# Five layers in one kernel: cross attention and layer 2 under one written TensorE order over five items, with shared PSUM pairs

## The chip, the cores and the metric

The kernel runs on one core of one Trainium2 chip. The time is the device time of one execution in microseconds (us); the kernel's time is the median over its runs. The inputs lie in device memory at the start, and the program is one launch.

In this text PE is TensorE, DVE is VectorE, ACT is ScalarE, POOL is GpSimd and SP is the engine that issues most DMAs.

## The reference, cut to what matters

The input `x` has 8 batches of 256 tokens by 320 channels; `ctx_768` holds 120 context tokens of 192 channels for each batch. Five blocks follow each other on the same `x`: a block with quantised attention and a feed-forward layer (L0), a plain transformer block (L1: self attention, cross attention, feed-forward), an attention on text and image tokens (L2), and a last attention (L3). All is float32 with softmax over scores.

The change touches the cross attention of L1 and all of L2:

```python
# L1, cross attention (20 heads of 16)
h2 = _ln(x, n2_g, n2_b)
x = _attn(h2, context, q2, k2, v2, o2_w, o2_b, heads) + x
# L2: 104 text tokens and 16 image tokens, softmax for each set
q = (hidden_states @ Wq).reshape(B, S, H, D)
out = _attend(q, k, v, scale)
out_ip = _attend(q, k_ip, v_ip, scale)
out = (out + IP_SCALE * out_ip).reshape(B, S, C)
out = out @ Wo + bo
return out + residual
```

## The kernel before, in words

`x` stays in SBUF as 16 tiles of 128 tokens; a batch is two of them (`TPB`). L0's attention runs first, in stages of its own. From there on the kernel is one flow of 40 items, which `run_flow` interleaves: 4 feed-forward items of L0 (512 tokens each), then for each of the 8 batches one item of self attention, then 8 of cross attention, 4 of L1's feed-forward, 8 of L2, and 8 of the last attention.

An attention item has four generators: `project`, `tops`, `out` and a fourth that ends the output projection. At each step of `run_flow`, item `step + 1` does its `tops`, item `step + 2` its `project`, item `step - 1` its last part and item `step` its `out`; the generators are advanced in turn, one piece each. So four batches are in flight, and the engines' order comes from this interleaving and from the framework, which places the instructions on each engine's queue and adds the semaphores. PE's order is not fixed by hand except inside a feed-forward item (`behind`).

For cross attention (`kind == "cross"`) and L2 (`kind == "both"`), keys and values of the context were computed earlier and lie in DRAM (`kd`, `vd`). One item does this:

- `project`: normalises the batch (cross only; DVE L314 to L322), turns it by six PE transposes (`turned`, L339) into `xT` with ACT evacuation (L341, L343 or L347), loads keys and values by DMA (L523, L524), and computes the queries in one PSUM pair (`duo`, L132 for 128 rows, L139 for 64 rows), which ACT puts into `qT` (`put_q`, L360, L362). The 20 heads are padded to 32 rows and stand as five groups (`G`) of four, so a matmul with 32 rows runs for four heads side by side.
- `tops` (`max_scores`, L394, then DVE's maxima, L401): scores with tokens on the partitions, only for the negated maximum of each row. Two groups share two PSUM pairs (`per = 512 // (2 * 120) = 2`). Then PE turns the maxima (L418), ACT copies them into `nT` (L419), and SP writes them by DMA into spare rows of `qT` (L422), five DMAs for cross, ten for L2, so that the next scores come out with the maximum taken off.
- `out` (`weighted`): scores with keys on the partitions (L439), two groups in two pairs, ACT's exponential into `e` (L445), the product with the values and the sums with a matrix of ones (L456) in a single PSUM bank, DVE's reciprocal and product (L464, L465) into `oT`. Cross adds two groups in one bank; L2 has one group in a bank, with text and image in the two halves of a head's 32 rows.
- the output projection (`project_out_steps`): POOL adds the bias to `x` (L487), PE multiplies by the weights for each half of the tokens (L120; three chunks for cross, five for L2), DVE adds the result to `x` (L493).

PSUM has two pools: `pair()` gives one of 3 tiles of two banks (`pf` in the profile) and `bank()` one of 2 tiles of one bank (`pa`).

Of the kernel before, what the change touches and what calls it, by code (L numbers as in the profile page):

```python
# [2 lines left out]

# [8 lines left out]
F32 = mybir.dt.float32  # L12
BF16 = mybir.dt.bfloat16
AF = mybir.ActivationFunctionType
ALU = mybir.AluOpType
AX = mybir.AxisListType
PSUM = bass.MemoryType.PSUM

P = 128
B, N, C = 8, 256, 320  # L20
NT = B * N // P
TPB = N // P
M, CC = 120, 192
# [9 lines left out]
H, D, PAD = 20, 16, 32  # L33
G = H * PAD // P
NIP = 16
NTXT = M - NIP
# [18 lines left out]
class Kernel:  # L55
# [56 lines left out]
    def bias_row(self, pool, i):  # L112
        t = pool.tile([P, C], F32, tag="brow", name="brow", bufs=3)
        self.nc.scalar.dma_start(t, self.a["rows"][i : i + 1, :].to_broadcast([P, C]))
        return t

    def mm(self, out, pairs):

        for i, (l, r) in enumerate(pairs):
            self.nc.tensor.matmul(out, l, r, start=i == 0, stop=i == len(pairs) - 1)  # L120
# [39 lines left out]
    def open_flow(self, ctx):  # L160
        nc, tc = self.nc, self.tc
        self.ps_f = ctx.enter_context(tc.tile_pool(name="ps_f", bufs=3, space=PSUM))
        self.ps_a = ctx.enter_context(tc.tile_pool(name="ps_a", bufs=2, space=PSUM))
        self.fw = ctx.enter_context(tc.tile_pool(name="f_weights", bufs=1))
        self.fk = fk = ctx.enter_context(tc.tile_pool(name="f_keep", bufs=1))
        self.work = ctx.enter_context(tc.tile_pool(name="f_work", bufs=2))

        self.m32 = fk.tile([P, PAD], F32, name="m32")
        nc.vector.tensor_reduce(self.m32, self.ident.rearrange("p (j r) -> p r j", r=PAD), AX.X, ALU.add)
        self.half = fk.tile([P, 2], F32, name="half")  # L170
        nc.vector.tensor_reduce(self.half, self.m32.rearrange("p (s r) -> p s r", s=2), AX.X, ALU.add)

        self.magic = fk.tile([P, 4], F32, name="magic")
        nc.gpsimd.memset(self.magic[:, 0:1], MAGIC)
        nc.gpsimd.memset(self.magic[:, 1:2], -MAGIC)
        nc.vector.tensor_scalar(self.magic[:, 2:4], self.half, -MAGIC, None, ALU.mult)
        self.count = 0

    def open_quant(self, pool):

# [327 lines left out]
    def heads_item(self, b, ln, w, brow, kind):  # L508

        nc = self.nc  # L510
        it = {}

        def project():
            xT = self.work.tile([P, 3, N], F32, tag="xT", name="xT")
            self.normed_T(b, xT, 0, ln)
            it["q"] = qT = self.hp.tile([P, G, N], F32, tag="qT", name="qT", bufs=3)
            nk = N if kind == "self" else M
            kT = self.hp.tile([P, G * N], F32, tag="kT", name="kT", bufs=3)[:, : G * nk]
            it["k"] = kT = kT.rearrange("p (g k) -> p g k", k=nk)
            it["v"] = v = self.vs[self.count % 3]  # L520
            self.count += 1
            if kind != "self":
                nc.sync.dma_start(kT, self.kd[kind][:, b])  # L523
                nc.sync.dma_start(v[:M, 0], self.vd[kind][:M, b])  # L524
            yield
            two = lambda wt, m, n: [self.by_weight(wt[i], xT, m[i], i) for i in range(n)]
            yield
            if kind == "self":
                for n, put in (("q", lambda p: self.put_q(qT, p)), ("k", lambda p: self.put_k(kT, p))):
                    ps = self.pair()  # L530
                    self.duo([ps[:, m, :N] for m in range(2)], two((w[n], w[n]), (0, 1), 2))
                    put(ps[:, :, :N])
                    yield
                ps = self.pair()
                self.duo([ps[:, i, :N] for i in range(2)], two((w["q"], w["k"]), (2, 2), 2))
                self.put_q(qT, None, ps[:, 0, :N])
                self.put_k(kT, None, ps[:, 1, :N])
                yield
                ps = self.pair()
                self.duo([ps[:, t, :C] for t in range(TPB)], [self.by_token(w["v"], xT, t, t) for t in range(TPB)])  # L540
                self.put_v(v, ps[:, :, :C])
                return
            ps = self.pair()
            outs, terms = [ps[:, m, :N] for m in range(2)], two((w["q"], w["q"]), (0, 1), 2)
            last = [ps[:, 0, N:]], two((w["q"],), (2,), 1)
            self.duo(outs, terms)
            self.half_rows(*last, False, False)
            yield
            self.whole_rows(*last, False, True)
            self.put_q(qT, ps[:, :, :N], ps[:, 0, N:])  # L550

        def tops():
            segs = [(0, N)] if kind == "self" else [(0, M)] if kind == "cross" else [(0, NTXT), (NTXT, M)]
            yield from self.top_scores(it["q"], it["k"], segs[-1][1], segs)

        def out():
            both = kind == "both"

            def oT():
                if "oT" not in it and both:  # L560
                    t = self.hp.tile([P, 4, 512], F32, tag="big", name="oT2", bufs=4)
                    it["oT"] = t.rearrange("p a n -> p (a n)")[:, : G * N].rearrange("p (g n) -> p g n", n=N)
                elif "oT" not in it:
                    it["oT"] = self.work.tile([P, 3, N], F32, tag="oT", name="oT", bufs=1)
                return it["oT"]

            kc, ks = (TPB, P) if kind == "self" else (1, M)
            yield from self.weighted(it["q"], it["k"], it["v"], kc, ks, both, oT)
            it["out"] = self.project_out_steps(b, it["oT"], w["o"], brow, self.bank)
            next(it["out"])  # L570

        return project, tops, out, lambda: it["out"]

    def ff_item(self, blk, ln, which, func, w, brow):
        nc = self.nc
# [99 lines left out]
    def run_flow(self, items, before={}, after={}):  # L675


        n = len(items)
        made = {}
        for step in range(-2, n + 1):  # L680
            if step + 2 < n:
                if step + 2 in before:
                    before[step + 2]()
                made[step + 2] = items[step + 2]()
            order = ((step + 1, 1), (step + 2, 0), (step - 1, 3), (step, 2))
            gens = [made[i][k]() for i, k in order if 0 <= i < n]
            while gens:
                for g in list(gens):
                    try:
                        next(g)  # L690
                    except StopIteration:
                        gens.remove(g)
            if step in after:
                after[step]()

# [254 lines left out]
    def last_item(self, b, w, brow, to):  # L950
# [3 lines left out]
        nc = self.nc  # L954
        HT = H3 * T3
        scale = D3 ** -0.5
        it = {}

        def project():
            x = self.x[:, TPB * b : TPB * (b + 1), :]  # L960
            xT = self.work.tile([P, 3, N], F32, tag="xT", name="xT")
            self.turned(x, xT, 0)
            qT = it["q"] = self.hp.tile([P, G3, N], F32, tag="qT", name="qT3", bufs=3)
            kz = self.hp.tile([P, G * N], F32, tag="kT", name="kz", bufs=3)
            kT = it["k"] = kz[:, : G3 * K3].rearrange("p (g k) -> p g k", k=K3)
            z = it["z"] = kz[:, 512 : 512 + 2 * N].rearrange("p (g n) -> p g n", n=N)
            vu = self.vs[self.count % 3].rearrange("p t h d -> p (t h d)")
            self.count += 1
            v = it["v"] = vu[:, : H3 * PAD3].rearrange("p (h d) -> p h d", d=PAD3)
            u = it["u"] = vu[:, 512 : 512 + TPB * H3 * PAD].rearrange("p (t h r) -> p t h r", h=H3, r=PAD)  # L970
            cs = it["c"] = w["pool"].tile([P, 2, CC], F32, tag="cs", name="cs", bufs=3)
# [18 lines left out]
            ps = self.pair()  # L990
# [12 lines left out]
            ps = self.pair()  # L1003
            wz = w["z"].rearrange("p c h r -> p c (h r)")
            self.duo([ps[:, g, :N] for g in range(2)], [self.by_weight(wz, xT, g, g) for g in range(2)])
            for c, t in ((2, 0), (2, 1), (0, 0), (1, 0), (0, 1), (1, 1)):
                o, nh = N + 3 * c * HT, 4 if c < 2 else 2
                rows = slice(64 * t, 64 * (t + 1)) if c == 2 else slice(0, P)
# [3 lines left out]
                    skip_group_check=True,  # L1012
# [624 lines left out]
def kernel(ctx: ExitStack, tc: tile.TileContext, a, out):  # L1637
    k = Kernel(ctx, tc, a, out)
    with ExitStack() as es:
# [12 lines left out]
        w, brow, loaded, w3 = {}, {}, {}, {}  # L1652
        dram = es.enter_context(tc.tile_pool(name="ahead", bufs=1, space=bass.MemoryType.DRAM))
        ff = ExitStack()
        with tc.tile_pool(name="l0", bufs=1) as pool:
            k.open_quant(pool)
            with tc.tile_pool(name="l0_keys", bufs=1, side="right") as kpool:
                s = Quant(k, pool, kpool, 0, *load("L0", "Wq1", "Wk1", "Wv1", "Wo1", 0), False)
                k.load_ctx()
                s.project_all()  # L1660
                c = Quant(k, pool, pool, 1, *load("L0", "Wq2", "Wk2", "Wv2", "Wo2", 1), True)
# [6 lines left out]
                n = len(s.units)  # L1668
# [4 lines left out]
                v = c.values_all()  # L1673
# [60 lines left out]

        items = [lambda i=i: k.ff_item(i, 2, 0, AF.Gelu_apprx_tanh, loaded["w"], brow["ff0"]) for i in range(4)]
        items += [lambda b=b: k.heads_item(b, 3, w["self"], brow["self"], "self") for b in range(B)]
        items += [lambda b=b: k.heads_item(b, 4, w["cross"], brow["cross"], "cross") for b in range(B)]
        items += [lambda i=i: k.ff_item(i, 5, 1, AF.Gelu, loaded["w1"], brow["ff1"]) for i in range(4)]
        items += [lambda b=b: k.heads_item(b, None, w["both"], brow["both"], "both") for b in range(B)]
        items += [lambda b=b: k.last_item(b, w3, brow["last"], out) for b in range(B)]  # L1740
        before = {12: load_cross, 24: load_both}
        k.run_flow(items, before, {
# [80 lines left out]
```

## Time and profile before

| | us |
|---|---|
| median of 3 runs | 2204.13 |
| the runs | 2198.03, 2204.13, 2205.01 |
| span of the profiled execution | 2202.1 |

The page gives no other time for the profiled execution than its span; the span is 2.0 us under the median of the runs.

In the profile, an instruction's line is the line of the helper that records it; `out<-in` are the program's names. PEld is PE's weight load. One float32 matmul is shown as two records, so `x8` of a 32-row matmul is four heads once. A group's "idle before" is the time its engine stood idle just before it, with what ended that. PEclk is the granted TensorE clock as a share of full speed.

In the trace of before the feed-forward of L0 runs from about 650 us, self attention from about 960, cross attention from about 1230, the feed-forward of L1 from about 1425, L2 from about 1714 and the last attention from about 1925 to the end.

### The profile page before, as it was taken

To read this page: it belongs to the slowest core of one execution; us is meant where nothing else is said; L and a number is where in the kernel's file an instruction comes from. 1 tells how busy PE (TensorE), PEld (TensorE's weight loads), DVE (VectorE), ACT (ScalarE), POOL (GpSimd) and SP (SyncE) were. 2 spreads that over 40 slices of the span, in tenths; PEclk is the share of its full clock that TensorE was granted. 3 is DMA by queue.
4 is the path that set the end of the run, shared out by engine and by line. 5 is a ranking of instruction groups with operands and counts; after the bars stand their busy time and mean duration, and the time that the engine had idled before them with its cause. 6 is when DMAs were issued, how large, how long until landed. Compare 5 with 4: busy or idle time off the path is not lost.

```text
span 2202.1 us, 38254 instructions
## 1 busy us (share of the span) xinstructions
PE 2036.4 (92%) x16415; PEld 1194.6 (54%) x16415; DVE 1112.6 (51%) x1698; ACT 833.3 (38%) x1259; POOL 330.5 (15%) x358
## 2 busy tenths in 40 slices
PE   7888889898889999999999998899999999999997
PEld 5643345554444465465555555544555655666664
DVE  5388687445651222235555567621121666546565
ACT  3456888367542121124444444311201333222221
POOL 3194033723010000000000010100000100000100
PEclk9989889898899999999999999999999999999999
DMA  4000000642120000020000101100000120000000
GB/s 118 20 12 2 2 1 1 174 111 57 52 85 14 1 0 1 1 93 2 2 2 22 28 25 36 47 1 0 1 0 1 24 68 23 19 16 26 23 19 16
DMA packets 79303, 63.21 MB, mean 29 GB/s; under 512 B 48410, under 2 KB 68318, under 8 KB 78622
## 3 DMA queue, kind: packets, MB, share of 16 engines
q1 hardware_dynamic: 75070, 57.06, 9.4%
q10 hardware_dynamic: 4064, 3.71, 0.6%
q8 instruction: 129, 2.11, 0.4%
q14 instruction: 40, 0.33, 0.0%
HBM read 42.61 MB, written 17.37 MB: 27 GB/s over the span
## 4 chain that ended last, share of the span: by engine, by line
PE 73%; DVE 15%; issue 4%; ACT 4%; POOL 2%; DMA 2%; SPq 0%; ACTq 0%; DVEq 0%; POOLq 0%
PE pf L594 13%; PE pf L120 11%; PE pf L132 9%; PE pa L120 7%; PE pa L456 6%; PE pf L439 4%; PE pa L594 3%; PE pf L139 3%; DVE negm L1456 3%; PE pf L394 3%; PE pf L736 3%; DVE rs L464 3%; PE pf L1497 2%; PE pa L1519 2%; DVE negm L401 2%
## 5 line engine op out<-in xcount | busy, mean ns | idle before, releaser
L445 ACT ACTIVATE e<-pf 128x1024 f32<-128x1024 f32 (+2 forms) x176 | 158.5, 946 | 220.1 <-PE pf L439 213.1
L401 DVE TENSOR_REDUCE negm<-pf 128x4 f32<-128x1024 f32 (+4 forms) x224 | 188.1, 887 | 97.9 <-PE pf L394 97.9
L594 PE MATMUL pf<-xTf,ff 128*128 128x512 f32 x512 | 230.8, 597 | 6.2 <-DVE negm L401 5.2
L464 DVE RECIPROCAL rs<-pa 128x256 f32<-128x256 f32 x88 | 152.3, 1745 | 143.5 <-PE pa L456 143.5
L1504 ACT ACTIVATE e<-pf,sc_s 128x1024 f32<-128x1024 f32 x160 | 169.8, 1118 | 48.7 <-PE pf L1497 44.8
L1456 DVE TENSOR_REDUCE negm<-pf 128x4 f32<-128x1024 f32 (+2 forms) x128 | 143.3, 1151 | 69.6 <-PE pf L1453 58.2
L619 DVE SCALAR_TENSOR_TENSOR hT<-pf,cols_sb,gl 128x512 f32<-128x512 f32 x64 | 48.0, 751 | 256.4 <-ACT gl L618 254.1
L120 PE MATMUL pf<-ff,hT 128*128 128x320 f32 x640 | 174.4, 434 | 0.0
L594 PEld LDWEIGHTS pf<-xTf,ff 128*128 128x128 f32 x512 | 94.3, 190 | 125.4 <-issue 118.5
L120 PEld LDWEIGHTS pf<-ff,hT 128*128 128x128 f32 x640 | 120.9, 190 | 55.5 <-issue 6.1
L618 ACT ACTIVATE gl<-pf,cols_sb 128x512 f32<-128x512 f32 x64 | 44.0, 689 | 247.8 <-PE pf L594 247.8
L439 PE MATMUL pf<-qT,kT 32*128 32x256 f32 (+1 forms) x1280 | 122.1, 410 | 9.1 <-DVE negm L401 7.5
L394 PE MATMUL pf<-kT,qT 32*128 32x120 f32 (+1 forms) x1920 | 113.1, 326 | 18.6 <-ACT e L445 18.3
L487 POOL TENSOR_TENSOR xb<-x_sb,brow 128x640 f32<-128x640 f32 x24 | 37.0, 1543 | 563.8 <-DVE x_sb L493 555.4
L120 PE MATMUL pa<-o,oT 128*128 128x320 f32 x352 | 105.7, 441 | 15.2 <-DVE oT L465 15.2
L394 PEld LDWEIGHTS pf<-kT,qT 32*128 32x128 f32 x1920 | 83.0, 186 | 58.4 <-ACT e L445 27.5
L647 POOL TENSOR_TENSOR xb<-x_sb,brow 128x640 f32<-128x640 f32 x16 | 25.0, 1563 | 573.8 <-DVE x_sb L652 528.2
L1497 PE MATMUL pf<-Q,K 32*128 32x256 bf16 (+1 forms) x960 | 90.5, 295 | 21.7 <-DVE negm L1456 11.5
L456 PE MATMUL pa<-e,v 128*32 128x256 f32 (+1 forms) x1280 | 106.1, 391 | 2.3 <-ACT e L445 1.7
L1606 DVE TENSOR_SCALAR w<-e 128x1024 bf16<-128x1024 f32 (+2 forms) x128 | 89.2, 703 | 32.3 <-ACT e L1504 31.1
L132 PE MATMUL pf<-xT,q 128*128 128x256 f32 x384 | 100.5, 391 | 0.4 <-ACT e L445 0.2
L439 PEld LDWEIGHTS pf<-qT,kT 32*128 32x128 f32 (+1 forms) x1280 | 68.4, 182 | 55.5 <-DVE negm L401 26.9
(291 smaller groups left out, 3439.2 us busy)
## 6 DMA issues: line engine op xcount, KB each, us to landing
ff<-in_L_xattn_Wff_dram SPq DMA_DIRECT2D x1, 2560.0 KB
qT<-nT SPq DMA_DIRECT2D x160, 4.0 KB
ff<-in_L_xattn_ff_w_dram SPq DMA_DIRECT2D x1, 2560.0 KB
out_dram<-x_sb SPq DMA_DIRECT2D x16, 160.0 KB
kd_cross<-kst SPq DMA_DIRECT2D x8, 300.0 KB
vd_cross<-vst SPq DMA_DIRECT2D x8, 300.0 KB
vd_both<-vst SPq DMA_DIRECT2D x8, 300.0 KB
kT<-kd_cross SPq DMA_DIRECT2D x8, 300.0 KB
```

The costliest lines, as they stand in the source:

```text
L120: self.nc.tensor.matmul(out, l, r, start=i == 0, stop=i == len(pairs) - 1)
L132: self.nc.tensor.matmul(o, *t[c], start=start and c == 0, stop=stop and c == n - 1, skip_group_check=True)
L394: nc.tensor.matmul(s[j // 2][:, j % 2, o : o + nk], qT[r : r + PAD, g, t * P : (t + 1) * P], kT[r : r + PAD, g, :nk], start=True, stop=True,)
L401: nc.vector.tensor_reduce(negm[:, n, 2 * i : 2 * i + 2, g0 : g0 + len(gs), :].rearrange("p j g t -> p j (g t)"), sv[:, :, :, k0:k1], AX.X, ...
L439: nc.tensor.matmul(s[j // 2][:ks, j % 2, o : o + N], kT[r : r + PAD, g, c * ks : (c + 1) * ks], qT[r : r + PAD, g, :], start=True, stop=True,)
L445: nc.scalar.activation(e[:ks, 2 * i : 2 * i + 2, :n], s[i][:ks, :, :n], AF.Exp, scale=scale)
L456: nc.tensor.matmul(o[j * PAD : (j + 1) * PAD, what * N : (what + 1) * N], w, es[g][:ks, j, c * N : (c + 1) * N], start=first and c == 0 an ...
L464: nc.vector.reciprocal(rs, o[:, N:])
L594: ins = nc.tensor.matmul(*args, **kw)
L1456: nc.vector.tensor_reduce(negm[:, 2 * h : 2 * h + 2, gs[0] : gs[-1] + 1, :].rearrange("p j g t -> p j (g t)"), s[:, :, : len(gs) * TPB * n ...
L1497: nc.tensor.matmul(s[at // 2][:ks, at % 2, o : o + N], l, m, start=not shift and o == 0, stop=shift and o + N == n, skip_group_check=True,)
L1504: nc.scalar.activation(e[:ks, :, :n], ps[:ks, :, :n], AF.Exp, scale=self.sc[:ks, 9:10])
```

## The change

Cross attention and L2 no longer use `heads_item`, but `context_item`. It has no generators for parts; it has one plan that says what the item does in each of five steps (d = -3 to 1), each step in five rounds with two halves, A and B. `in_order` records PE's instructions of these pieces and chains them, so that PE follows the written order exactly.

In half A of a round PE computes exponent scores of one group of item `i` (`exps(g)`, columns 256 to 511 of two pairs) and then the maximum scores of one group of item `i + 1` or `i + 2` (`tops(g)`, columns 0 to 239 of the same two pairs, from `shared_pairs`). In half B come the other products: values, queries, the turned maxima, output projection, transposes. Maxima and exponentials are now taken for each group by itself. The queries are one burst of 64-row matmuls and one of 128-row ones, the output projection one burst into a pair with one addition on DVE.

`run_flow` goes in steps from -3, makes each item one step earlier, and advances a context item in both halves of a round and any other item in half B alone. `self.count`, which picks the value buffer, is now taken when the item is made.

```diff
+    @contextmanager
+    def in_order(self):
+        traced = self.nc.cur_bb.bb.instructions
+        start = len(traced)
+        yield
+        order = mybir.DependencyInfo(mybir.DependencyClass.NoSync, mybir.DependencyReason.DATA)
+        for i in traced[start:]:
+            if i.engine == mybir.EngineType.PE:
+                if self.last_pe is not None:
+                    self.tc.add_manual_dep(i, self.last_pe.name, order, reason="order on the engine")
+                self.last_pe = i
...
+    def shared_pairs(self):
+        if self.shared is None:
+            self.shared = [self.pair() for _ in range(2)]
+        return self.shared
+
+    def context_item(self, b, ln, w, brow, kind):
...
+        def queries():
+            it["q"] = qT = self.hp.tile([P, G, N], F32, tag="qT", name="qT", bufs=3)
+            two = lambda m: [self.by_weight(w[kind]["q"], it["xT"], j, i) for i, j in enumerate(m)]
+            ps = self.pair()
+            first, last = ([ps[:, m, :N] for m in range(2)], two((0, 1))), ([ps[:, 0, N:]], two((2,)))
+            self.half_rows(*first, True, False)
+            self.half_rows(*last, False, False)
+            self.whole_rows(*first, False, True)
+            self.whole_rows(*last, False, True)
+            self.put_q(qT, ps[:, :, :N], ps[:, 0, N:])
+
+        def tops(g):
...
+            s = self.shared_pairs()
+            for t in range(TPB):
+                for j in range(4):
+                    r = j * PAD
+                    nc.tensor.matmul(
+                        s[j // 2][:, j % 2, t * M : (t + 1) * M], qT[r : r + PAD, g, t * P : (t + 1) * P],
+                        kT[r : r + PAD, g, :], start=True, stop=True,
+                    )
+            for i in range(2):
+                sv = s[i][:, :, : TPB * M].rearrange("p j (t k) -> p j t k", k=M)
+                for n, (k0, k1) in enumerate(segs):
+                    nc.vector.tensor_reduce(
+                        negm[:, n, 2 * i : 2 * i + 2, g, :], sv[:, :, :, k0:k1], AX.X, ALU.max, negate=True
+                    )
...
+        def exps(g):
+            if g % 2 == 0:
+                it["e"] = self.hp.tile([P, 4, 512], F32, tag="big", name="e", bufs=4)
+            e = it["e"][:, :, g % 2 * N : (g % 2 + 1) * N]
+            s = self.shared_pairs()
+            for j in range(4):
+                r = j * PAD
+                nc.tensor.matmul(
+                    s[j // 2][:M, j % 2, N:], it["k"][r : r + PAD, g, :], it["q"][r : r + PAD, g, :],
+                    start=True, stop=True,
+                )
+            for i in range(2):
+                nc.scalar.activation(e[:M, 2 * i : 2 * i + 2, :], s[i][:M, :, N:], AF.Exp, scale=scale)
+            es[g] = e
...
+        def project_out():
+            po, wo = self.pair(), w[kind]["o"]
+            for t in range(TPB):
+                self.mm(po[:, t, :C], [(it["oT"][:, c, t * P : (t + 1) * P], wo[:, c, :]) for c in range(wo.shape[1])])
+            nc.vector.tensor_tensor(xs, po[:, :, :C], it["xb"], ALU.add)
...
+        plan = {
+            -3: {"A1": [norm], "B4": [turn, keys]},
+            -2: {"B0" if both else "B1": [queries], "B2": [context_values], "A3": [one(tops, 0)], "A4": [one(tops, 1)]},
+            -1: {"A0": [one(tops, 2)], "A1": [one(tops, 3)], "A2": [one(tops, 4)], "B3" if both else "B2": [rows]},
+            0: {f"A{g}": [one(exps, g)] for g in range(G)} | {"B2": [one(values, (0, 1))], "B4": [one(values, (2, 3))]},
+            1: {"B1" if both else "B0": [one(values, (4,))], "A2": [biased], "B3": [project_out]},
+        }
...
-        for step in range(-2, n + 1):
...
-            order = ((step + 1, 1), (step + 2, 0), (step - 1, 3), (step, 2))
-            gens = [made[i][k]() for i, k in order if 0 <= i < n]
+        for step in range(-3, n + 1):
...
+            for d in (0, -1, -2, 1, -3):
+                i = step - d
+                if 0 <= i < n and callable(made[i]):
+                    gens.append(made[i](d))
+            for d, k in ((-1, 1), (-2, 0), (1, 3), (0, 2)):
+                i = step - d
+                if 0 <= i < n and not callable(made[i]):
+                    gens.append(halves(made[i][k]()))
             while gens:
...
+                self.shared = None
+                for _ in range(2):
+                    for g in list(gens):
+                        try:
+                            next(g)
+                        except StopIteration:
+                            gens.remove(g)
...
-        items += [lambda b=b: k.heads_item(b, 4, w["cross"], brow["cross"], "cross") for b in range(B)]
+        items += [lambda b=b: k.context_item(b, 4, w, brow, "cross") for b in range(B)]
...
-        items += [lambda b=b: k.heads_item(b, None, w["both"], brow["both"], "both") for b in range(B)]
+        items += [lambda b=b: k.context_item(b, None, w, brow, "both") for b in range(B)]
```

## The prediction

> **What bounds the kernel now.** I read the page first, for the engines' shares, then windows over four steady steps of each touched stage (cross attention of layer 1, layer 2), then the timeline of one step, and last windows around a drop of TensorE's clock.
>
> ```profile
> PE 2036.4 (92%) x16415; PEld 1194.6 (54%) x16415; DVE 1112.6 (51%) x1698; ACT 833.3 (38%) x1259; POOL 330.5 (15%) x358
> ```
> ```profile
> core 0: us, PE busy (x) PEld busy (x) DVE busy (x) ACT busy (x) POOL busy (x), PEclk, DMA share, GB/s
> 1266.21:1356.33 90.12, 82.60 (x956) 51.58 (x952) 61.34 (x85) 35.53 (x56) 8.97 (x9) 1.00 0.11 30
> 1746.53:1847.77 101.24, 92.90 (x1000) 59.30 (x992) 68.51 (x96) 33.24 (x56) 8.16 (x10) 1.00 0.19 51
> ```
>
> PE is the busiest engine everywhere. Four cross steps take 90.12 us, so one batch costs 22.53 us; four steps of layer 2 take 101.24, so 25.31 each. PE is busy for nine tenths of both windows, DVE for 68%, ACT for 39 and 33%. But "busy" includes the tails of pipelined matmuls, so PE's real work must come from start to start:
>
> ```profile
> 1310.84 0.61 PE L456 MATMUL pa<-e,ones 120*32 120x256 f32 x8
> ...
> 1311.39 0.72 PE L394 MATMUL pf<-kT,qT 32*128 32x120 f32 x16
> ...
> 1312.04 1.99 PE L132 MATMUL pf<-xT,q 128*128 128x256 f32 x8
> ...
> 1313.96 1.13 PE L139 MATMUL pf<-xT,q 64*128 64x256 f32 x6
> ...
> 1315.02 1.14 PE L439 MATMUL pf<-qT,kT 32*120 32x256 f32 x16
> ...
> 1319.23 0.69 PE L439 MATMUL pf<-qT,kT 32*120 32x256 f32 x4
> ...
> 1320.03 0.60 ACT L445 ACTIVATE e<-pf 120x512 f32<-120x512 f32 x1 [0.25 <-PE pf L439]
> ...
> 1328.94 1.94 ACT L445 ACTIVATE e<-pf 120x1024 f32<-120x1024 f32 x2 [2.21 <-PE pf L439]
> ...
> 1330.02 1.15 PE L394 MATMUL pf<-kT,qT 32*128 32x120 f32 x28 [0.79 <-ACT e L445]
> ```
>
> One fp32 matmul is two records, and four heads run side by side, so eight records are one "quad". The x8 burst of L456 holds PE for 0.55 us until the next kind begins (1310.84 to 1311.39); where the next burst is of the same kind the same timeline has 0.43 (1298.74 to 1299.17 to 1299.60). A quad of 256 columns is thus 0.43, and a change of kind costs between 0.1 and 0.2. L132 x8 takes 1.92, some 0.2 over 8 x 0.216, the spacing inside such a burst. I use 0.2 per change. The 16 records of L394 (two quads of 120 columns) take 0.65 with their change: 0.45 without. The last three lines price a hand-over to ACT and back: ACT starts 0.80 after the first of these scores (1319.23 to 1320.03), an exponential over 512 columns takes 0.60, and PE starts again 0.11 after the first of two 0.97 us exponentials (1328.94 + 0.97 = 1329.91, then 1330.02).
>
> PE's work in a cross step: exponent scores 5 x 0.43 = 2.15; maximum scores 5 x 0.45 = 2.25; values and sums 10 x 0.43 = 4.3; queries 12 x 0.216 for the whole rows and 2 x 0.43 for the halves (two side by side, then one) = 3.45; transposes 0.65 and 0.25; output projection 12 x 0.269 = 3.23 (an x80 burst of L120 takes 21.7). Sum 16.3. In layer 2 the projection has 20 records (5.38) and the rows 0.5: 18.7. A step of before has some 15 changes of kind, 3.0. So before waits about 22.53 - 16.3 - 3.0 = 3.2 us in a cross step and 25.31 - 18.7 - 3.0 = 3.6 in layer 2. That and the changes are all that an order of PE's can win.
>
> **The change, part by part.** *Longer bursts.* Queries become one burst of halves and one of wholes, the projection one burst, values two groups at a time. The new step has 13 changes of kind: 13 x 0.2 = 2.6, a gain of 0.4. With no wait left a step would be 16.3 + 2.6 = 18.9 and 18.7 + 2.6 = 21.3.
>
> *Smaller pieces on DVE and ACT.* Maxima go from three groups of up to 960 columns to five of 480. The lines by form have 1.15 and 0.64 us, so 4 x 1.15 + 2 x 0.64 = 5.9 becomes 10 x 0.64 = 6.4. Exponentials go from 4 x 0.97 + 2 x 0.60 = 5.1 to 10 x 0.60 = 6.0. Neither engine is near a step's length: DVE has 61.34/4 = 15.3 and 68.51/4 = 17.1, so I cost this at nothing while PE's steps stay over 20; if they fell to 18.9, DVE's 16 would be nearly late.
>
> *Shared pairs.* This decides. In each of five rounds A, `exps(g)` of one batch writes columns 256 to 511 of four PSUM banks, two pairs, and `tops` of another batch then writes columns 0 to 239 of the same banks. Each pair's exponential reads its own banks in between. In the order in which the changed kernel is built, the first maximum matmul in each pair waits for ACT, namely for the exponential of this very round on this very pair. On PE everything stands in one fixed order, so the rest of tops, and all of half B (values, queries, rows, projection, transposes), is queued behind that wait. From the first score of a round: ACT starts at 0.80 and ends the first exponential at 1.40, PE does two heads from 1.51; the second ends at 2.00 and PE does the rest from 2.11. Without the wait PE would go on at 0.43. The price is 2.11 - 0.43 = 1.68 a round, 8.4 a step.
>
> The Trainium skill states why such a wait must be there ("PSUM — Partial Sum Buffer", section "PSUM bank collisions raise a hardware error"): two engines that touch one bank and the same 32 partitions at once, even in different columns, raise an error, and nothing stalls them, so the program has to. It speaks against this change; by it the rounds cost the 8.4, and without it the steps would be the 18.9 and 21.3 above.
>
> *ACT's own queue lengthens two rounds.* The transposes end half B4, and their four copies stand ahead of the first exponential: they begin 0.92 after the transposes (1301.24 to 1302.16) and last 2.04, until 2.96, where the exponential would begin at 0.76 + 0.80 = 1.56: +1.4. Layer 2's copies are shorter (from 0.91 to 2.14 after the transposes begin, 1785.27 to 1787.41): +0.6. The round after the queries waits for their three evacuations, 1.27 + 0.37 = 1.64 from about 0.35 after the last query matmul, to 2.0, where the exponential would begin at 0.9: +1.1. In layer 2 the rows need one of the two PSUM banks that values still hold until two reciprocals (1.75 each) and a product (0.42) are through on DVE, 3.9 after the last value matmul, while round A3 between them takes PE 2.6: +1.3.
>
> Steps after: cross 16.3 + 2.6 + 8.4 + 1.4 + 1.1 = 29.8, that is +7.3; layer 2 18.7 + 2.6 + 8.4 + 0.6 + 1.1 + 1.3 = 32.7, +7.4. The tops beside an exps belong to the next two batches, so of 40 rounds in a stage 33 have a partner (the last batch has none, the one before only three): 6.6 steps pay, 1.4 run without waits and win 22.53 - 18.9 = 3.6 and 4.0. Cross: 6.6 x 7.3 - 1.4 x 3.6 = 43. Layer 2: 6.6 x 7.4 - 1.4 x 4.0 = 43. Together +86.
>
> *The clock.* Where PE idles, its clock falls:
>
> ```profile
> 1211.90:1215.31 3.41, 1.92 (x17) 0.99 (x16) 2.35 (x3) 1.70 (x4) 0.00 (x0) 1.00 0.00 0
> 1215.31:1218.73 3.42, 3.42 (x34) 1.38 (x32) 0.00 (x0) 1.77 (x2) 0.00 (x0) 0.50 0.00 0
> 1641.98:1645.39 3.41, 2.01 (x35) 1.42 (x35) 2.02 (x3) 0.00 (x0) 0.00 (x0) 1.00 0.00 0
> 1645.39:1648.80 3.41, 3.41 (x16) 1.46 (x14) 0.34 (x2) 0.00 (x0) 0.00 (x0) 1.00 0.00 0
> ```
>
> A stretch of 3.41 us with 1.92 busy is followed by one at clock 0.50, one with 2.01 is not. The two lengthened rounds leave PE idle for 2.3 and 2.0 us on end (first tops at 1.51 + 1.4 or + 1.1, less the 0.6 for which the scores still show busy), and 1.5 idle in one stretch is enough. A fixed grid of 3.41 catches that about three times in four: 13 steps x 2 x 0.75 = 20 slow stretches. Each costs between 0 (if PE waits anyway) and 1.7 (half of it); I take 1.0: +20, bounds 0 and +45 (26 x 1.7).
>
> A rule of the Trainium skill says otherwise ("TensorE: Matmul & The Clock Gate", section "HAM oscillation"): what matters is that no idle gap exceeds about 3.4 us. No wait here is so long, so by it this term is 0 and the sum 2290. The row with 1.92 busy, where no gap was over 1.1 us, speaks against it.
>
> *The ends.* Flow items now span five steps, `made` runs a step earlier, and other items advance in half B only, in their old order. The last batch of a stage leaves its fifth group and projection to one step more, at most a reciprocal, a product and a projection, 1.75 + 0.42 + 5.4 = 7.6, with the next items beside it: 0, bounds 0 and +15. Key and value loads move past the rows' DMAs on SP; these need 2.9 and 5.7 us of issue in steps of 30, so 0.
>
> Sum: 43 + 43 + 20 = +106 against the profiled span of 2202.1, which lies 2.0 below the median of the runs, 2204.1: 2310.
>
> **Rivals.** (1) *The wait is there, but most of it was paid before too, as the 3.2 and 3.6 us that PE waits now.* With 0.4 left of each round's 1.68 the sum is 86 - 66 x 1.28 = +2 and the clock stays up: 2206. For it: PE's share of before has such waits (0.79 on ACT above). Against: 0.80 and 0.60 are measured on this very form, and the 3.2 is already taken off above. (2) *PE streams on*: if the exponentials do not hold the maximum matmuls back, steps are 18.9 and 21.3, 3.6 and 4.0 less over 8 batches each, -61: 2143. This is the faster side; it decides once a round's wait is under 1.68 - 86/66 = 0.38 us. For it: work and changes are counted from rows, and nothing is computed more often. Against: the built wait. (3) *DVE falls behind too*: a pair comes free only after its two maxima, and reciprocals of 1.75 stand in that queue. If one more reciprocal ended late per step, 13 x 2 x 1.75 = +46: 2356. For it: the rows' bank wait above. Against: DVE has 16 to 18 us of work in 30.
>
> **How the numbers follow.** Forecast 0.84, rival 1 0.03, rival 2 0.05, rival 3 0.08. About 0.3% is what a measurement of this kernel can tell from no change (the three runs lie within 7 us). Low end: the 86 at four fifths, no clock loss: 2272, and a margin for rival 1's direction: 2265. High end: clock at 45 and one end of 5: 2340. Faster 0.06, same 0.01, slower 0.93.
>
> **What would show it.** In the profile after: steps of about 30 and 33 us; in the waits, PE's maximum scores released by ACT's exponential, some 66 rounds (33 per stage) of about 1.1 and 0.6 us; fewer than nine tenths of PE busy in both stages; PEclk under 1 in them; self attention and both feed-forward stages unchanged. Wrong if the tops start within 0.7 us of the exps, or if steps are under 25 us.

## The result and the profile after

The changed kernel takes 2306.0 us (median of four runs, 2301.8 to 2310.0) where the kernel before takes 2201.1 beside it: 1.048 times as long, with a 95% interval of 1.045 to 1.050, or +105 us. The profiled execution has a span of 2301.6 (before 2202.1: +99.5). The forecast was 2310, between 2265 and 2340.

Busy times on the page, and windows over four steps of each touched stage (cross attention, then layer 2):

```profile
PE 2099.3 (91%) x16415; PEld 1227.8 (53%) x16415; DVE 1109.8 (48%) x1778; ACT 838.6 (36%) x1323; POOL 330.3 (14%) x358
```
```profile
1310.88:1439.24 128.36, 105.51 (x956) 63.29 (x958) 61.82 (x97) 36.94 (x72) 9.37 (x9) 0.85 0.10 25
1861.16:1989.23 128.07, 108.27 (x1010) 67.76 (x1013) 68.02 (x121) 35.40 (x72) 9.18 (x13) 0.96 0.11 31
```

The page alone would hide the matter: PE is 91% busy where it was 92%. The windows show it. Four cross steps went from 90.12 to 128.36 us and four of layer 2 from 101.24 to 128.07; PE's busy share in them fell from 92% to 82 and 85%, and its clock from 1.00 to 0.85 and 0.96. PE issued the same 16415 matmuls.

An ordinary round, the round behind the transposes and the one behind the queries, in the timeline of one cross step (start, length, engine, line; in brackets the idle time before it and who ended it; L675 exponent scores, L680 exponentials, L644 maximum scores, L701 values, L353 and L361 transposes and their copies):

```profile
1344.61 0.71 PE L675 MATMUL pf<-qT,kT 32*120 32x256 f32 x8
...
1345.41 1.08 ACT L680 ACTIVATE e<-pf 120x512 f32<-120x512 f32 x2 [4.92 <-PE pf L675]
...
1346.06 1.19 PE L644 MATMUL pf<-kT,qT 32*128 32x120 f32 x16 [0.74 <-ACT e L680]
...
1346.54 0.52 PEld L644 LDWEIGHTS pf<-kT,qT 32*128 32x128 f32 x12 [0.19 <-ACT e L680]
...
1347.18 0.64 PE L701 MATMUL pa<-e,v 120*32 120x256 f32 x8
...
1349.85 0.71 PE L675 MATMUL pf<-qT,kT 32*120 32x256 f32 x8
1349.96 2.04 ACT L361 ACTIVATE xT<-pf,cols_sb 128x256 f32<-128x256 f32 x4 [3.47 <-PE pf L353]
...
1352.02 1.09 ACT L680 ACTIVATE e<-pf 120x512 f32<-120x512 f32 x2
...
1352.67 1.20 PE L644 MATMUL pf<-kT,qT 32*128 32x120 f32 x16 [2.11 <-ACT e L680]
...
1361.15 0.71 PE L675 MATMUL pf<-qT,kT 32*120 32x256 f32 x8
...
1363.34 1.19 PE L644 MATMUL pf<-kT,qT 32*128 32x120 f32 x16 [1.48 <-ACT e L680]
```

In the first round ACT starts 0.80 after the scores, the maximum scores start 1.45 after them, the weight loads of twelve of their sixteen records wait until 1.93, and the next work starts at 2.57. In the second the four copies stand ahead of the exponential, and the maximum scores start at 2.82; in the third they start at 2.19. The waits of the whole execution (total, times, longest) name the same pair of lines. First the kernel before (its line holds self attention too), then the changed kernel, with 65 waits where some 66 were forecast, and last PEld, the weight load of the same matmuls, whose waits run beside PE's and are not to be added to them:

```profile
PE pf L394 <- ACT e L445: 18.3, 22, 1.0
```
```profile
PE pf L644 <- ACT e L680: 64.4, 65, 2.1
```
```profile
PEld pf L644 <- ACT e L680: 102.7, 119, 2.5
```

The granted clock, read in windows on its own grid of 3.41 us (PE busy is the second number, the clock the third from the end):

```profile
1361.91:1365.33 3.42, 1.99 (x32) 1.37 (x36) 0.87 (x2) 1.86 (x5) 0.00 (x0) 1.00 0.00 0
1365.33:1368.74 3.41, 3.41 (x30) 1.25 (x22) 1.76 (x2) 0.36 (x1) 0.00 (x0) 0.50 0.00 0
...
1378.99:1382.40 3.41, 1.30 (x15) 0.70 (x15) 2.48 (x4) 2.83 (x6) 0.00 (x0) 1.00 0.00 0
1382.40:1385.82 3.42, 3.42 (x36) 1.82 (x36) 1.22 (x2) 0.28 (x1) 0.00 (x0) 0.50 0.00 0
```

1361.91 is the round behind the queries, 1378.99 the one behind the transposes: each leaves PE busy for less than 2 us of a stretch, and the next stretch runs at half clock. After 640 us of the span, 108.9 us lie at half clock, against 22.8 before: 86 more, or 25 stretches. In the touched stages there are 26, where before has none; they come in 15 falls, of which ten last one stretch and the others two to five.

### The profile page after: what moved, and what is told of

Same layout as the page of the kernel before. It is cut to its first block, busy times and chain, and to the rows that moved or that the text cites. A ratio compares the mean times of both kernels' runs of the same rounds, so it can differ in the third digit from the quotient of the medians.

```text
span 2301.6 us, 38527 instructions
## 1 busy us (share of the span) xinstructions
PE 2099.3 (91%) x16415; PEld 1227.8 (53%) x16415; DVE 1109.8 (48%) x1778; ACT 838.6 (36%) x1323; POOL 330.3 (14%) x358
## 5 line engine op out<-in xcount | busy, mean ns | idle before, releaser
L651 DVE TENSOR_REDUCE negm<-pf 128x4 f32<-128x416 f32 (+1 forms) x240 | 102.9, 484 | 143.2 <-PE pf L644 142.7
L644 PE MATMUL pf<-kT,qT 32*128 32x120 f32 x1280 | 95.4, 320 | 66.7 <-ACT e L680 64.4
L680 ACT ACTIVATE e<-pf 120x512 f32<-120x512 f32 x160 | 87.7, 598 | 170.0 <-PE pf L675 167.6
L644 PEld LDWEIGHTS pf<-kT,qT 32*128 32x128 f32 x1280 | 67.6, 196 | 115.1 <-ACT e L680 102.7
L706 DVE RECIPROCAL rs<-pa 128x256 f32<-128x256 f32 x64 | 110.2, 1741 | 32.3 <-PE pa L701 32.3
L415 DVE TENSOR_REDUCE negm<-pf 128x4 f32<-128x1024 f32 x80 | 94.3, 1218 | 53.1 <-PE pf L408 53.0
L811 POOL TENSOR_TENSOR xb<-x_sb,brow 128x640 f32<-128x640 f32 x16 | 25.0, 1562 | 569.7 <-DVE x_sb L816 519.4
L1685 ACT ACTIVATE e<-pf,sc_c 120x1024 f32<-120x1024 f32 (+1 forms) x96 | 88.3, 980 | 28.6 <-PE pf L1678 26.8
L459 ACT ACTIVATE e<-pf 128x1024 f32<-128x1024 f32 x80 | 77.5, 1022 | 55.4 <-PE pf L453 52.6
L145 PEld LDWEIGHTS pf<-xT,q 128*128 128x128 f32 x384 | 76.7, 208 | 24.1 <-issue 11.8
L1678 PE MATMUL pf<-nTs,sel 32*128 32x256 bf16 (+1 forms) x960 | 85.2, 287 | 4.2 <-DVE nTs L1751 4.2
```

The costliest lines, as they stand in the source:

```text
L145: self.nc.tensor.matmul(o, *t[c], start=start and c == 0, stop=stop and c == n - 1, skip_group_check=True)
L415: nc.vector.tensor_reduce(negm[:, n, 2 * i : 2 * i + 2, g0 : g0 + len(gs), :].rearrange("p j g t -> p j (g t)"), sv[:, :, :, k0:k1], AX.X, ...
L644: nc.tensor.matmul(s[j // 2][:, j % 2, t * M : (t + 1) * M], qT[r : r + PAD, g, t * P : (t + 1) * P], kT[r : r + PAD, g, :], start=True, s ...
L651: nc.vector.tensor_reduce(negm[:, n, 2 * i : 2 * i + 2, g, :], sv[:, :, :, k0:k1], AX.X, ALU.max, negate=True)
L680: nc.scalar.activation(e[:M, 2 * i : 2 * i + 2, :], s[i][:M, :, N:], AF.Exp, scale=scale)
L706: nc.vector.reciprocal(rs, o[:, N:])
```

## The experiments

The theory is that the exponential's reading of a pair holds back the maximum scores in the same banks, and PE with them. The rivals are that this wait only takes the place of older ones, that the loss is the fixed order or the longer bursts, and that DVE's maxima are what comes late. Ratios are to the kernel before, run beside each.

**e1: no reader on ACT's side.** The exponentials read a constant from SBUF, so their values are not those of the scores; number, form and place stay.

```diff
-                nc.scalar.activation(e[:M, 2 * i : 2 * i + 2, :], s[i][:M, :, N:], AF.Exp, scale=scale)
+                src = self.ident[:M].unsqueeze(1).unsqueeze(1).to_broadcast([M, 2, 2, P])
+                nc.scalar.activation(
+                    e[:M, 2 * i : 2 * i + 2, :].rearrange("p a (b k) -> p a b k", k=P), src, AF.Exp, scale=scale
+                )
```

> The exponentials of both stages read a constant in SBUF instead of the scores in PSUM (same size and count, the result of the attention is left out), so no engine but DVE reads a shared bank and the maximum scores need not wait for ACT. Theory 1, the wait for the round's own exponential on the same banks carries the loss: the 66 waiting rounds lose their 1.68 us, cross steps fall from 29.6 to about 20, layer 2 from about 32 to about 25, PE's maximum scores no longer wait for ACT, and the time is 2150 to 2205. Theory 2, the written order itself makes PE wait (each piece stands behind another one that is late): the ACT wait is replaced by another, and the time stays over 2270. Theory 3, DVE's reciprocals release the pairs late: over 2270 too.

Measured: 2194.9, ratio 0.997 (0.994 to 0.999), 9.5 us under the kernel before. The loss is gone, so the wait is its cause. But of the gain that a flow without the wait was to bring (61 us, rival 2) little is there. Windows over four cross steps (the stretches at half clock in it lie in the last step; the three steps before that take 19.70 each) and over one step of layer 2 at full clock, and the wait that is left:

```profile
1324.53:1403.53 79.00, 75.44 (x916) 49.98 (x919) 58.50 (x93) 33.49 (x65) 9.44 (x9) 0.96 0.16 40
1804.98:1829.91 24.93, 21.12 (x252) 14.39 (x255) 17.15 (x31) 8.96 (x19) 1.56 (x1) 1.00 0.10 28
```
```profile
PE pa L661 <- DVE oT L710: 15.3, 6, 2.7
```

A cross step is 19.75 (18.9 forecast for no wait), a layer 2 step 24.93 (21.3 forecast): of those 3.6, about 2.5 are the rows (L661) waiting for the bank that the values still hold. The forecast had 1.3 for that, and only in the version that waits for ACT.

**e2: no reader on DVE's side.** The maxima read a constant from SBUF (the shift of the exponent is then a constant too).

```diff
-                        negm[:, n, 2 * i : 2 * i + 2, g, :], sv[:, :, :, k0:k1], AX.X, ALU.max, negate=True
+                        negm[:, n, 2 * i : 2 * i + 2, g, :],
+                        self.hundred.unsqueeze(1).unsqueeze(1).to_broadcast([P, 2, TPB, k1 - k0]),
+                        AX.X, ALU.max, negate=True,
```

> The maxima of both stages read a constant in SBUF instead of the scores in PSUM (same size and count, the true row maximum is left out); the exponentials read PSUM as in the changed kernel. Theory 1: the maximum scores still write banks that the exponential of the round reads, so the waits stay; 2285 to 2320. Theory 3 (DVE holds the pairs): the pairs come free without DVE, so 2240 to 2265. Theory 2: no change, like theory 1.

Measured: 2311.1 in two runs, ratio 1.049 (1.041 to 1.057), the changed kernel's within that interval. No cost of the maxima shows where they stand, and rival 3 falls.

**e3 and e4: one stage alone.** Only cross attention, then only layer 2, gets the new item; the other keeps the old one (shown for e3; e4 does the same to cross attention).

```diff
-        items += [lambda b=b: k.context_item(b, None, w, brow, "both") for b in range(B)]
+        items += [lambda b=b: k.heads_item(b, None, Late(w, "both"), Late(brow, "both"), "both") for b in range(B)]
```

> Cross attention has the new item, layer 2 the old one (its weights are looked up a step later, since items are now made earlier). By the prediction's sum cross attention carries 43 of 86 us and about half of the clock's 20: 2254, range 2235 to 2275. If one stage carried the loss, 2205 or 2305.

> Layer 2 has the new item, cross attention the old one. By the prediction's sum 43 of 86 and half of the clock's 20: 2254, range 2235 to 2275; together with the kernel that has the new cross attention alone the two differences should add up to about 105.

Measured: 2266.6, ratio 1.029 (1.023 to 1.035), and 2248.7, ratio 1.020 (1.015 to 1.026): +62 and +44 against the 2204.3 beside them. The two sum to +106, the whole loss as far as the intervals (some 12 us to each side) can tell, so nothing shows that the stages disturb each other. The split of the forecast (53 each) was even; cross attention carries more.

**e5: without the written order.** PE's instructions get no order beyond what the scheduler gives them.

```diff
-                if self.last_pe is not None:
+                if False:
```

> The changed kernel without the chain on PE: the framework places PE's instructions again, the shared pairs, the plan and the sizes stay. Theory 1 (the wait is on the shared banks, whatever the order): the maximum scores still need the round's exponential, only other matmuls may slip in between; 2255 to 2310. Theory 2 (the written order makes PE wait): back to 2195 to 2225.

Measured: 2291.7, ratio 1.042 (1.040 to 1.044), +93 against the 2198.5 beside it. The written order is worth some 12 to 14 of the 105 us. PE's maximum scores still wait for the exponentials 61 times, 50.2 us in all.

**e6: the maximum scores after half B.** A third part C of each round takes the tops, so that values, queries and projection lie between the two kinds of scores.

```diff
-            -1: {"A0": [one(tops, 2)], "A1": [one(tops, 3)], "A2": [one(tops, 4)], "B3" if both else "B2": [rows]},
+            -1: {"C0": [one(tops, 2)], "C1": [one(tops, 3)], "C2": [one(tops, 4)], "B3" if both else "B3": [rows]},
...
-                for p in "AB":
+                for p in "ABC":
```

> Each round gets a third part C: the maximum scores come after the other products of half B, so that the exponential runs beside them. If the wait can be hidden by work in between, each round gains up to 1.68 and the time is 2190 to 2220. Theory 1 in full (two readers share the banks, so hiding ACT's turn exposes DVE's): the next round's exponent scores follow the maximum scores at once and must wait for their two maxima, 0.64 each behind reciprocals of 1.75, so the 1.7 us come back on DVE: 2280 to 2345, with PE's exponent scores released by DVE.

Measured: 2339.1, ratio 1.064 (1.062 to 1.066), slower still; steps of layer 2 are 37 to 38. The waits say where it went:

```profile
PE pf L675 <- DVE negm L651: 49.1, 39, 2.9
```

The exponent scores of the next round now come right behind the tops and wait until DVE has read the same banks, while the tops' wait for ACT falls from 64.4 us to 1.3. Two readers share each bank, and hiding the one exposes the other. This moves the wait more than it adds to it: what makes e6 slower than the changed kernel, by 33 us, is most likely the clock: 176.5 us lie at half against 108.9, or 20 stretches more, 30 us at the 1.5 us a stretch of the account below.

**e7: a pair for each kind.** Exponent scores and maximum scores get pairs of their own, filled with two groups at a time (six rounds); the order is written out on DVE too.

```diff
-            s = self.shared_pairs()
+            s = [self.pair() for _ in range(2)]
+            for n, g in enumerate(gs):
...
-            for r in range(G):
+            for r in range(6):
```

> Written order (on PE and on DVE) and long bursts stay, but exponent scores and maximum scores get pairs of their own again, two groups at a time, in six rounds whose score parts alternate between the two kinds with other products between them. Theory 1: no bank has two kinds of readers, an evacuation runs beside the products of the round; steps of about 20 and 25 us, 2175 to 2210. Theory 2: over 2280.

Measured: 2191.6, ratio 0.998 (0.996 to 1.000), 5% under the changed kernel. The first four steps are 19.4 to 22.9 in cross attention and 24.3 to 25.6 in layer 2, and PE's maximum scores wait for an exponential of these stages 4 times, 2.3 us in all. So the five-step flow, the written order and the bursts can be had without a loss. That the shared pairs are what costs does not follow from e7 alone, since its pieces are larger too; e1, which keeps the pieces and the pairs and takes away the one reader, shows it.

**e8, e10, e11: the bursts alone.** The kernel before with its queries (e10), its output projection (e11, into a pair), or both (e8) as one burst.

```diff
-            self.duo(outs, terms)
+            self.half_rows(outs, terms, True, False)
...
-            yield
+            self.whole_rows(outs, terms, False, True)
...
+            yield
```

```diff
+        po = self.pair()
+        n = oT.shape[1]
+        for t in range(TPB):
+            self.mm(po[:, t, :C], [(oT[:, c, t * P : (t + 1) * P], wo[:, c, :]) for c in range(n)])
+        nc.vector.tensor_tensor(x, po[:, :, :C], xb, ALU.add)
```

> The kernel before with the long bursts alone: in cross attention and layer 2 the queries are one burst of halves and one of wholes, and the output projection is one burst into a pair with one addition. By the prediction's sum two changes of kind less per step: 16 x 0.4 = 6 us less, 2198. Against it: the projection takes a pair from the three that scores need, and a burst of 3.2 to 5.4 us leaves ACT and DVE without scores, so that PE waits for them later: up to 2240.

> The kernel before with one part of the burst run alone: the queries' halves and wholes as one burst each, the projection as before. Both bursts together lost 32 us. If the loss is from holding PE in one piece while ACT's scores wait for their pair, both parts lose, this one (3.4 us held) less than the projection (3.2 to 5.4 us held and a pair taken): about 2210, +10. If it comes from the projection taking a pair of the three that scores use, this one loses nothing: 2198 to 2203.

> The kernel before with the other part alone: the output projection as one burst into a pair, queries as before. If the loss is from the pair taken, nearly all of the 32 us is here: 2228. If both bursts lose by holding PE, about 2220.

Measured: both 2230.6, ratio 1.014 (1.012 to 1.016), +32; queries 2210.7, ratio 1.004 (1.001 to 1.007), +6 by the medians and +9 by the ratio; projection 2217.6, ratio 1.007 (1.004 to 1.010), +13 and +16. Each burst loses by itself, by about what the expectation of holding PE gave. PE's waits show for what: two lines of the kernel before, one of e10, two of e11:

```profile
PE pa L120 <- DVE oT L465: 15.2, 14, 1.9
...
PE pa L456 <- ACT e L445: 1.7, 5, 0.7
```
```profile
PE pa L456 <- ACT e L445: 10.9, 29, 0.7
```
```profile
PE pf L120 <- DVE negm L401: 12.0, 5, 2.4
...
PE pf L120 <- ACT xT L343: 7.9, 6, 1.3
```

With the queries in one piece, the values (L456) wait for the exponential 29 times in place of 5, 9.2 us more, about the loss. The projection (L120) waits for its pair until DVE has read the maxima, 12.0 us, and until ACT has copied the transposes, 7.9 us, two waits that the kernel before does not have; of its old wait for `oT`, 15.2 us, there is 1.1 left. These are waits for the pair taken, so for the projection the time fits the one expectation and the wait the other, and which of the two it is stays open. So in the old flow the 0.4 us a step that the forecast gave to fewer changes of kind is more than taken back; that the short pieces were the cover of these waits is how I read it, and no run shows it.

**e9: evacuations off ACT's queue.** In the changed kernel, DVE copies the transposes and the queries, in both touched stages.

```diff
-            self.turned(it["x"], it["xT"], 0, ln)
+            self.turned(it["x"], it["xT"], 0, ln, on_v=True)
...
-            self.put_q(qT, ps[:, :, :N], ps[:, 0, N:])
+            for s in range(2):
+                nc.vector.tensor_scalar(qT[:, s:4:2, :], ps[:, :, :N], self.half[:, s : s + 1], None, ALU.mult)
+            nc.vector.tensor_copy(qT[:, 4, :], ps[:, 0, N:])
```

> The changed kernel with the evacuations of the transposes and of the queries on DVE in place of ACT, in cross attention and layer 2 alone; all else as changed. If ACT's queue is what lengthens two rounds of each step, as the prediction has it (+1.4 and +1.1, of which the trace shows 1.4 and 0.8 in cross, 0.6 and 0.8 in layer 2), the first maximum scores of these two rounds start about 1.4 us after the first exponent scores again, steps fall from 29.6 to about 27.4 and from 30.2 to about 28.8, and the stretches at half clock, which came from the two long idle stretches, mostly go: some 24 us from the rounds and 10 to 15 from the clock, 2265 to 2275. If the half clock comes from the waits of all rounds alike, only the first part comes: about 2282. Rival (DVE late): the evacuations and the 1.75 us reciprocals stand in one queue with the maxima, the pairs come free later and the gain is eaten: 2300 or more, with new waits of the exponent scores on DVE's maxima.

Measured: 2281.2, ratio 1.038 (1.032 to 1.043): some 22 to 25 us less than the changed kernel (by ratio and by medians), nearer to the 2282 expected for the rounds alone than to the 2265 to 2275 with the clock. That nearness means little, for the timeline has both theories at work, one in each stage. In cross attention the round behind the transposes is like any other:

```profile
1379.89 0.71 PE L684 MATMUL pf<-qT,kT 32*120 32x256 f32 x8
1380.69 1.09 ACT L689 ACTIVATE e<-pf 120x512 f32<-120x512 f32 x2 [4.16 <-PE pf L684]
...
1381.34 1.20 PE L653 MATMUL pf<-kT,qT 32*128 32x120 f32 x16 [0.74 <-ACT e L689]
```

The maximum scores start at 1.45 again, four steps in a row take 25.9, and none of them has a stretch at half clock. In layer 2 the copies stand behind two reciprocals on DVE, and the queries, which come next there, wait for them:

```profile
1849.50 1.60 PE L152 MATMUL pf<-xT,q 64*128 64x256 f32 x6 [1.47 <-DVE xT L358]
```

There steps take 31.9 to 33.6, two stretches at half clock in most of them, and next to nothing is won. This is the rival's case in that the copies come late on DVE, though what waits is the queries and not, as the rival had it, the exponent scores.

## Why the prediction was right, and where it only came out right

**The mechanism stands.** A round with a partner waits for its own exponential, PE starts the maximum scores at 1.45 (forecast 1.51), and without that reader (e1) the loss is gone. The rule that the prediction took from the Trainium skill ("PSUM — Partial Sum Buffer", section "PSUM bank collisions raise a hardware error") agrees with the row: columns 0 to 239 wait for a reader of columns 256 to 511 of the same bank. What would happen without the wait no run here shows.

**The sum came out right by terms that were not.** The rounds were over-sized, the clock under-sized, and that the two nearly cancel is luck. The steps that can be compared are those without a stretch at half clock. In cross attention that is e9's 25.9 plus the two lengthened rounds as the changed kernel has them, 2.82 - 1.45 and 2.19 - 1.45, together 2.1: 28.0, a figure put together and not one step read off. In layer 2 it is the step from 1894.70 to 1924.88: 30.2.

| term | forecast | measured |
|---|---|---|
| cross step, full clock | 29.8 | 28.0 |
| layer 2 step, full clock | 32.7 | 30.2 |
| 6.6 of each, 1.4 without partner | +86 | about +58 to +64 |
| stretches at half clock | 20 at 1.0 | 25 at about 1.5 |
| the clock's term | +20 | about +38 |
| ends, as what is left | 0 | within 4 of 0 |
| sum, against the span | +106 | +99.5 |

The third row is 86 less 6.6 x (1.8 + 2.5) = 28, so 58, if the 1.4 steps without a partner win the 3.6 and 4.0 of the forecast; with the 2.8 and 0.4 by which e1's steps are shorter than before it is 64.

*Rounds: over-sized.* The forecast makes a round 0.43 + 0.45 + 1.68 and two changes of kind of 0.2: 2.96. The trace has 2.57. Put otherwise, the forecast has 2.11 until the second exponential is done and 0.85 from there; the trace has 1.93 and 0.64. The two exponentials take 1.08 together, not twice 0.60, and 0.2 of work was counted on top of the wait that lies inside it: the first four of the sixteen records start at 1.45, and with them one change of kind. Five rounds of 0.39 are 2.0.

*ACT's queue: right, the parts a little large.* +1.4 behind the transposes was 1.37, +0.6 in layer 2 was 0.56, +1.1 behind the queries was 0.74. The rows' bank wait of +1.3 was 0.60 in the changed kernel. With these 0.4 in cross attention and 1.1 in layer 2, the parts say 2.4 and 3.1 under the forecast where the steps came in 1.8 and 2.5 under it; where the other 0.6 went I did not find.

*The clock: under-sized by half.* Each stretch cost some 1.5, not 1.0: the cross step with one stretch took 29.58 against 28.0, the layer 2 step with two 33.54 against 30.18, and over seven such steps the price is 1.2 to 1.7. That is nearly half of 3.41, the price of a stretch in which PE has work throughout. It has: the stretch that follows a long wait is the one in which PE catches up. The worst were steps where the fall met the query burst, whose wholes then took 5.21 us in place of 2.86; such steps took 33.9 and 35.3, with four and five stretches. The count of 20 came near to the 25 for another reason than the forecast's. It let the two lengthened rounds of each step make 20 falls of one stretch; there were 15 falls, some of several stretches, and five of them follow a stretch that no idle time of PE over 0.7 us touches, so not a lengthened round. The rule on idle gaps that the prediction set against its row ("TensorE: Matmul & The Clock Gate", section "HAM oscillation") would have made this term 0; PE was idle for no longer than 2.11 us at once in these stages, and 25 more stretches fell. The measurement decides against the rule. The 1.92 and 2.01 us of the prediction's rows are no threshold either, as the last section shows.

*The gain without a wait: not there.* Rival 2 would have been wrong even if its condition had held. e1 meets it and lies at 2195, not 2143. Its steps win 2.8 and 0.4 in place of 3.6 and 4.0, which over 8 batches is 35 us less; the layer 2 step kept a bank wait of 2.5. And e1 itself has ten more stretches at half clock than the kernel before (56.5 us against 22.8), some 15 us. In the forecast this gain was subtracted from a wait that was too dear; what a wait costs net, 28.0 - 19.7 = 8.3 a cross step and 30.2 - 24.9 = 5.3 in layer 2, is less than the 10.9 and 11.4 of the forecast.

*The ends: right, though the profile looks otherwise.* The first output of cross attention comes 22.8 us later than before. But in e1 it comes 16.7 later and the last one only 4.5 later: a batch takes one step more from start to end, and most of that is given back when the flow drains. Marks outside the touched stages show it: from the end of the fifth batch of self attention to the first addition of the second item of L1's feed-forward the kernel before takes 391.6 us, the changed kernel 449.8, e1 383.4; from there to the third batch of the last attention they take 483.0, 528.6 and 487.4. So cross attention carries +58 and layer 2 +46, near the +62 and +44 that e3 and e4 measured, and the terms give 53 (6.6 x 5.5 - 1.4 x 2.8 and 14 stretches of 1.5) and 50 (6.6 x 4.9 - 1.4 x 0.4 and 12).

Rival 1 falls with the steps: at full clock they went from 22.5 to 28.0 and from 25.3 to 30.2, so most of the wait is new; before had paid some 2.8 of the 8.3 a cross step and 0.4 of the 5.3 in layer 2, by which e1's steps are shorter. Rival 3 falls with e2.

## What to carry to other kernels

Before two kinds of products share a PSUM bank, list who reads each of them: PE comes back to the bank only after both, and moving the wait of one away (e6) brings up that of the other. A long burst saves changes of kind, but e8, e10 and e11 lost time by it, so look at what waits the shorter pieces may have covered. In a sum of waits, do not add what PE can do inside the wait, and price a fall of the clock at nearly half of each stretch, since PE is at work again when it comes, and allow for falls that last several.

## What the runs showed of the hardware

Neither the busy share of a stretch nor the longest gap in it says by itself whether the clock falls. In the rows above 1.30 and 1.99 us busy were followed by half clock, and before 1.92 was and 2.01 was not. But the changed kernel also has these two pairs of neighbours, which are the other way round:

```profile
1280.02:1283.43 3.41, 2.42 (x38) 1.59 (x38) 1.63 (x3) 1.40 (x3) 0.00 (x0) 1.00 0.06 14
1283.43:1286.85 3.42, 3.42 (x40) 1.55 (x34) 1.22 (x2) 0.00 (x0) 0.00 (x0) 0.50 0.32 86
...
1873.93:1877.35 3.42, 1.94 (x17) 1.15 (x15) 0.00 (x0) 2.36 (x5) 0.00 (x0) 1.00 0.00 0
1877.35:1880.76 3.41, 2.66 (x42) 1.38 (x42) 2.57 (x5) 0.92 (x3) 0.00 (x0) 1.00 0.25 55
```

In the first pair PE is 2.42 us busy, with no gap over 0.57, and the clock falls; in the second it is 1.94 us busy, with a gap of 1.48, and the clock stays. Over the 13 traces of this case, after 640 us, each of the 40 full-clock stretches with less than 1.5 us busy was followed by half clock, none with over 2.75, and in between 114 of 849. So less work makes a fall likelier, and what else decides stays open. Coming back is no plainer. After the fall at 1382.40 the clock stayed at half for four stretches though PE shows 2.73 to 3.42 us busy in each of them; ten of the 15 falls lasted one stretch. What decides on the return stays open, and no run here was made for it.
